# Two PSUM banks for the low-rank product, two copying engines, and gate and up in turns at the block heads

## The chip, the cores and the metric

The kernel runs on one NeuronCore of a Trainium2 chip. The metric is the device time of one execution in microseconds. Before the change it is 483.63 us (median of three runs, 483.47 to 484.6). The profile of one of these executions has a span of 481.9 us; times within the kernel count from the start of that span. The engines are TensorE (PE; its weight loads are PEld), VectorE (DVE), ScalarE (ACT), GpSimd (POOL) and SyncE (SP), which issues nearly all transfers.

## The reference

For each of 8 batches of 256 tokens of width 1024 there is an adapter, one of eight, picked by an index. It is a low-rank product: x times B (to 16 numbers per token), and that times A (back to 1024). Its result goes through a feed-forward part with fp8 rounding and comes back as an addition to x.

```python
Bx  = einsum('bni,bri->bnr', x, B[ids])        # 1024 -> 16
y   = einsum('bnr,bor->bno', Bx, A[ids])       # 16 -> 1024
q   = fp8(y / in_scale) * in_scale
hidden = silu(q @ gate.T * s_g) * (q @ up.T * s_u)    # 1024 -> 2752
return x + fp8(hidden / s_in) @ down.T * s_d           # 2752 -> 1024
```

All inputs are float32; the weights of gate, up and down already lie on the fp8 grid.

## The kernel before

The 2048 tokens are cut into four blocks `t` of 512 (two batches each), the 1024 inputs into eight slices `k` of 128, the 2752 hidden units into 22 chunks `c` of 128 (the last has 64). Everything lies transposed: features on partitions, tokens along the free axis. Products land in PSUM, of which a pool of eight banks (tag `ps`) hands out one at a time. Three stages follow each other.

**Low-rank product.** For blocks 0 and 1 `two_times_b` (line 445) forms B's product `bx` for a block: at each of the eight `k`, four matmuls of 128 tokens each go to the four groups of 32 rows of one bank; rows 0 to 63 hold one batch and rows 64 to 127 the other. Then `bx` is copied to SBUF as `bm`: one copy of all rows by DVE (line 454), and four copies of 16 rows, each into its neighbour's group of rows, two by DVE and two by ACT (line 459). `two_times_a` (line 470) multiplies by A in two parts. Each part fills four banks `c0` to `c3` with 16 matmuls (a float32 matmul leaves two records in the trace), the first eight with the plain copy and the others with the shifted ones. Each full bank is rounded to fp8 into `xg` by `round_to`: two banks by ACT (line 468) and two by DVE (line 466). A bank can be used again once it has been rounded. Blocks 2 and 3 share `four_times_b` and `four_times_a`, with 256 tokens a matmul.

**Gate and up.** `gate_up(c, t)` (line 519) runs eight matmuls of 512 tokens for gate and eight for up, each eight into a bank of its own (`y0`, `y1`), then ACT's SiLU on gate and DVE's multiplication with up (line 548), whose result is `hid`. For blocks 0 and 1 the slices `k` are taken in the order in which they are rounded:

```python
ORDER = [0, 1, 4, 5, 2, 3, 6, 7]
```

`between` is called after gate's matmuls and `halfway` after four of up's. Lines 571 to 593 use them to weave the low-rank product of the next block into gate and up of this one. `pass_time` runs matmuls on zeros so that TensorE doesn't stand still at the start.

**Down.** 22 chunks are summed into the output, x is added, and the block is written (lines 643 to 675).

**What sets the order.** Every engine works through its own queue in order. `multiply` and the copies are held in program order; the other instructions are placed by the tile layer, which also puts in the waits: a reader waits for the writer, a new user of a bank for its last reader, and an instruction of one engine for those of other engines on the same bank, reads included. SyncE issues the loads in the order of lines 343 to 369 and 598; the first chunk of `w_gu` is behind x of block 0, then come the other three of the first four chunks, block 1's adapters and x in two halves, and blocks 2 and 3.

Of the kernel before, what the change touches and what calls it, by code (L numbers as in the profile page):

```python
# [2 lines left out]

# [5 lines left out]
F32 = mybir.dt.float32  # L9
# [8 lines left out]
P = 128  # L18
T = 2048
SEQ = 256  # L20
# [3 lines left out]
R = 16  # L24
NH = H // P
NI = (I + P - 1) // P
TAIL = I - (NI - 1) * P
TB = 512
# [5 lines left out]
ORDER = [0, 1, 4, 5, 2, 3, 6, 7]  # L34
# [11 lines left out]
def high(ap):  # L46

    return ap.bitcast(BF16)[..., 1::2]
# [205 lines left out]
def adaln_ffn(  # L254
# [13 lines left out]
    nc = tc.nc  # L268
    const = ctx.enter_context(tc.tile_pool(name="const", bufs=1))
    psum = ctx.enter_context(  # L270
        tc.tile_pool(name="psum", bufs=8, space=bass.MemoryType.PSUM)
    )
# [16 lines left out]
    with ExitStack() as fast:  # L289
        acts = fast.enter_context(tc.tile_pool(name="acts", bufs=1))  # L290
        lora = fast.enter_context(tc.tile_pool(name="lora", bufs=1))
# [5 lines left out]
        xg = [acts.tile([P, NH, TB], FP8, name=f"xg{t}") for t in range(NTB)]  # L297
# [9 lines left out]
        b_two = [lora.tile([P, 2 * BROW + R], F32, name=f"b{t}") for t in range(2)]  # L307
        a_two = [lora.tile([P, H // 2], F32, name=f"a{t}") for t in range(2)]

        b_four = lora.tile([P, 4 * BROW + R], F32, name="b_four")  # L310
# [109 lines left out]
        def multiply(*args, **kwargs):  # L420
            tc.keep_in_program_order(nc.tensor.matmul(*args, **kwargs))  # L421
# [3 lines left out]
            for i in range(n):  # L425
                multiply(to[:, :P], lhsT=zeros, rhs=zeros, start=(i == 0), stop=(i == n - 1))

        def times_b(b, n, quads, between=None):

            bx = psum.tile([P, n], F32, tag="ps", name="bx")  # L430
            for k in range(NH):
                for q, (t, i, cols) in enumerate(quads):
                    at = i * BROW + k * R
                    multiply(
                        bx[32 * q : 32 * (q + 1)],
                        lhsT=b[:, at : at + 32],
                        rhs=xs[t][:, k, cols],
                        start=(k == 0),
                        stop=(k == NH - 1),
                    )  # L440
                if between:
                    between(k)
            return bx

        def two_times_b(t, between=None):


            n = SEQ // 2
            quads = [(t, q // 2, bass.ts(q, n)) for q in range(4)]
            bx = times_b(b_two[t], n, quads, between)  # L450
            bm = [
                lora.tile([P, n], F32, tag=f"bm{i}", name=f"bm{i}", bufs=2) for i in range(3)
            ]
            tc.keep_in_program_order(nc.vector.tensor_copy(bm[0], bx))
            for q in range(4):
                to = bm[1 + q // 2][32 * q : 32 * q + R]
                other = bx[32 * (q ^ 1) : 32 * (q ^ 1) + R]
                tc.keep_in_program_order(
                    nc.vector.tensor_copy(to, other) if q < 2 else nc.scalar.copy(to, other)  # L459
                )  # L460
            return bm

        def round_to(to, c, engine):
# [6 lines left out]
        def two_times_a(t, bm):  # L470

            n = SEQ // 2
            for part in range(2):
                cs = [psum.tile([P, 2, SEQ], F32, tag="ps", name=f"c{q}") for q in range(4)]
                for other in range(2):
                    for i in range(2):
                        for q in range(4):
                            rows = slice(32 * q, 32 * q + R)
                            multiply(
                                cs[q][:, i, bass.ts(q % 2 ^ other, n)],  # L480
                                lhsT=a_two[t][rows, bass.ts(2 * part + i, P)],
                                rhs=bm[other * (1 + q // 2)][rows],
                                start=True,
                                stop=True,
                            )
                for q in range(4):
                    k = 4 * (q % 2) + 2 * part
                    to = xg[t][:, k : k + 2, bass.ts(q // 2, SEQ)]
                    round_to(to, cs[q], nc.vector if q // 2 else nc.scalar)

        def four_times_b():
            quads = [(2 + q // 2, q, bass.ts(q % 2, SEQ)) for q in range(4)]
            bx = times_b(b_four, SEQ, quads)
            bm = lora.tile([P, SEQ], F32, tag="bm", name="bm", bufs=2)
            nc.vector.tensor_copy(bm, bx)
            return bm

        def four_times_a(bm, pairs):
            for i in pairs:
                cs = [psum.tile([P, 2, SEQ], F32, tag="ps", name=f"c{q}") for q in range(4)]  # L500
                for k in range(2):
                    for q in range(4):
                        rows = slice(32 * q, 32 * q + R)
                        multiply(
                            cs[q][:, k],
                            lhsT=a_four[rows, bass.ts(2 * i + k, P)],
                            rhs=bm[rows],
                            start=True,
                            stop=True,
                        )  # L510
                for q in range(4):
                    to = xg[2 + q // 2][:, 2 * i : 2 * i + 2, bass.ts(q % 2, SEQ)]
                    round_to(to, cs[q], nc.vector if q % 2 else nc.scalar)
# [2 lines left out]
            return slice(0, TAIL) if t % 2 else slice(TAIL, P)  # L516


        def gate_up(c, t, between=None, halfway=None):
            tail = c == NI - 1  # L520
            w = w_of[c]
            cols = bass.ts(t, TB)
            ys = []
            for j in range(1 if tail else 2):
                y = psum.tile([P, TB], F32, tag="ps", name=f"y{j}")
                order = ORDER if t < 2 else range(NH)
                for i, k in enumerate(order):
                    if halfway and j and i == NH // 2:
                        halfway()
                    multiply(  # L530
                        y,
                        lhsT=high(w[:, j * NH + k, :]),
                        rhs=xg[t][:, k, :],
                        start=(k == order[0]),
                        stop=(k == order[-1]),
                    )
                ys.append(y)
                if between and not j:
                    between()
            gates, ups = (ys[0], ys[-1]) if not tail else (ys[0][:TAIL], ys[0][TAIL:])  # L540
            rows = slice(TAIL, P) if tail else slice(0, P)
            if tail:
                to = lora.tile([P, 2 * TB], FP8, tag="bm", name="tail", bufs=2)[half_of(t), :TB]
            else:
                to = hid[c][:, cols]
            g = work.tile([P, TB], F32, tag="g", name="g")
            nc.scalar.activation(g[rows], gates, AF.Silu, scale=gate_s[: gates.shape[0]])  # L547
            nc.vector.scalar_tensor_tensor(  # L548
                to,
                in0=ups,  # L550
                scalar=up_by_down[rows],
                in1=g[rows],
                op0=ALU.mult,
                op1=ALU.mult,
                saturate=False,
            )
            if tail:
                nc.vector.tensor_copy(hid_tail[half_of(t), t // 2], to)
            if c > 1 and t == (NTB - 1 if c < 4 else 1):
                for done in {2: (0, 2), 3: (1, 3)}.get(c, (c,)):  # L560
                    note_low_bits(w_of[done], P, done)
                if c <= 1 + 2 * NTB:
                    i, half = divmod(c - 2, 2)
                    ks = slice(half * NH // 2, (half + 1) * NH // 2)
                    note_squares(xg[i][:, ks, :], P, c - 2)
                for done in (0, 1) if c == 2 else (c - 1,):
                    note_squares(hid[done], P, 2 * NTB + done)
# [5 lines left out]
        bm = two_times_b(0, lambda k: pass_time(warm, 6) if k in (3, 5) else None)  # L573
        pass_time(warm, 8)
        two_times_a(0, bm)
        for c in range(3):
            gate_up(c, 0)
        bms = []
        gate_up(
            3,  # L580
            0,
            between=lambda: bms.append(two_times_b(1)),
            halfway=lambda: two_times_a(1, bms[0]),
        )
        for c in range(2):
            gate_up(c, 1)
        gate_up(
            2,
            1,
            between=lambda: bms.append(four_times_b()),  # L590
            halfway=lambda: four_times_a(bms[1], (0, 1)),
        )
        gate_up(3, 1, between=lambda: four_times_a(bms[1], (2, 3)))
        for c in range(4):
            for t in (2, 3):
# [47 lines left out]
        for k in range(NH):  # L643
            ws = []
            for half in range(2):
                n = HALF - half
                w = wpool.tile([P, 2 * NH, P], F32, tag="w", name="w_d")[:, :n]
# [9 lines left out]
            for t in range(NTB):  # L657
                for c in range(NI - 1):
                    nc.tensor.matmul(  # L659
                        ys[t],  # L660
                        lhsT=high(ws[c]),
# [95 lines left out]
```

## Time and profile before

| | us |
|---|---|
| time, median of three | 483.63 |
| span of the profile | 481.9 |
| PE busy | 473.1 (98%) |
| ACT busy | 192.3 (40%) |
| DVE busy | 105.5 (22%) |
| one gate or up matmul, mean record | 0.379 |
| one rounding: ACT (line 468), DVE (line 466) | 0.686, 0.746 |
| copy of 16 rows: ACT, DVE (line 459) | 0.257, 0.281 |
| SiLU, multiplication into hid | 0.681, 0.751 |

A matmul's record of 379 ns is its latency. Matmuls overlap, so a row of them advances faster than that. Busy shares are means over the three stages; what an edit can do is read from the stretch where it works, here the first 56 us. The chain of waits goes back from the last instruction to what released each step, and shows which engine set the pace at each time.

### The profile page before, as it was taken

How to read it: one execution, taken by the hardware profiler on the slowest of the kernel's cores; microseconds unless marked ns; L12 is line 12 of the kernel's file. 1: busy time of each engine (PE TensorE's matmuls, PEld its weight loads, DVE VectorE, ACT ScalarE, POOL GpSimd, SP SyncE). 2: the span in 40 equal slices, each digit the busy share in tenths (PEclk: the TensorE clock that was granted, in tenths of full speed). 3: DMA queues.
4: the chain of work that ended last, by engine and by line, in shares of the span. 5: the costliest groups of instructions: out<-in, count | busy, mean ns of one | idle time of the engine just before them, and what ended most of it. 6: DMA issues, size and time to landing. Idle time of an engine off the chain costs nothing.

```text
span 481.9 us, 6062 instructions
## 1 busy us (share of the span) xinstructions
PE 473.1 (98%) x2550; PEld 221.3 (46%) x2550; DVE 105.5 (22%) x165; ACT 192.3 (40%) x247; POOL 0.2 (0%) x4
## 2 busy tenths in 40 slices
PE   8999999999999999999999999999999999999994
PEld 7554544444444444444444444444444444444442
DVE  1341521212121212121212121232120120111021
ACT  1331517995556654433454544359112112011000
POOL 0000000000000000000000000000000000000000
PEclk9999999999999999999999999999999999999999
DMA  8997004522221122222211111111434335242031
GB/s 287 418 345 243 1 0 148 194 97 88 87 88 48 46 82 89 87 87 88 87 37 52 45 60 55 61 54 62 151 116 137 115 131 158 76 170 99 0 133 50
DMA packets 13173, 52.67 MB, mean 109 GB/s; under 512 B 1554, under 2 KB 2578, under 8 KB 9554
## 3 DMA queue, kind: packets, MB, share of 16 engines
q1 hardware_dynamic: 12992, 52.14, 31.9%
q8 instruction: 22, 0.36, 0.3%
q14 instruction: 13, 0.11, 0.1%
q10 hardware_dynamic: 146, 0.07, 0.0%
HBM read 43.81 MB, written 8.39 MB: 108 GB/s over the span
## 4 chain that ended last, share of the span: by engine, by line
PE 95%; DVE 0%; ACT 0%; issue 0%
PE y L421 62%; PE yd L659 30%; PE c L421 1%; PE bx L421 1%; PE yd L627 1%; ACT xg L468 0%; DVE o L637 0%; DVE xg L466 0%; PE count L618 0%
## 5 line engine op out<-in xcount | busy, mean ns | idle before, releaser
L421 PE MATMUL y<-xg,w_gu 128*128 128x512 fp8e4 x1376 | 298.5, 379 | 0.1
L421 PEld LDWEIGHTS <-w_gu 128*128 128x128 bf16 x1376 | 133.9, 98 | 163.2 <-DVE xg L466 1.5
L659 PE MATMUL yd<-hid,w_d 128*128 128x512 fp8e4 x672 | 146.1, 379 | 0.0
L547 ACT ACTIVATE g<-y,gate_s 128x512 f32<-128x512 f32 (+1 forms) x88 | 59.8, 681 | 139.5 <-PE y L421 139.5
L548 DVE SCALAR_TENSOR_TENSOR hid<-y,up_by_down,g 128x512 fp8e4<-128x512 f32 x84 | 63.1, 751 | 218.5 <-PE y L421 153.5
L659 PEld LDWEIGHTS <-w_d 128*128 128x128 bf16 x672 | 65.3, 98 | 79.9 <-issue 1.7
L407 ACT ACTIVATE junk<-w_d 128x1408 bf16<-128x1408 uint16 (+1 forms) x16 | 21.2, 1324 | 88.5 <-DMA w_d<-w_d 88.4
L637 DVE SCALAR_TENSOR_TENSOR o<-yd,down_s,x 128x512 f32<-128x512 f32 x32 | 23.0, 748 | 118.1 <-PE yd L627 62.4
L407 ACT ACTIVATE junk<-w_gu 128x2048 bf16<-128x2048 uint16 (+1 forms) x22 | 41.0, 1864 | 0.1
L414 ACT ACTIVATE junk<-hid 128x2048 bf16<-128x2048 fp8e4 x21 | 40.0, 1905 | 0.4
L414 ACT ACTIVATE junk<-xg 128x2048 bf16<-128x2048 fp8e4 x8 | 15.2, 1905 | 0.2
L468 ACT ACTIVATE xg<-c,inv 128x512 fp8e4<-128x512 f32 x16 | 9.9, 686 | 7.2 <-PE c L421 7.2
L466 DVE TENSOR_SCALAR xg<-c,inv 128x512 fp8e4<-128x512 f32 x16 | 11.1, 746 | 6.6 <-PE c L421 6.5
L421 PE MATMUL warm<-zeros 128*128 128x128 bf16 x84 | 8.0, 278 | 1.0 <-DVE zeros L279 1.0
L421 PEld LDWEIGHTS <-zeros 128*128 128x128 bf16 x84 | 7.3, 131 | 1.6 <-DVE zeros L279 1.0
L421 PE MATMUL c<-bm,a 16*128 16x128 f32 x128 | 5.4, 287 | 0.6 <-ACT xg L468 0.6
L459 ACT COPY bm<-bx 16x128 f32<-16x128 f32 x4 | 1.0, 257 | 12.0 <-DMA w_gu<-w_gu 9.8
L421 PEld LDWEIGHTS c<-bm,a 16*128 16x128 f32 x128 | 4.8, 185 | 1.3 <-ACT xg L468 0.7
L421 PE MATMUL c<-bm,a_four 16*128 16x256 f32 x64 | 4.7, 394 | 0.3 <-ACT xg L468 0.3
L421 PE MATMUL bx<-x,b 128*32 128x128 f32 x128 | 4.3, 275 | 0.7 <-DMA x<-x 0.4
L407 ACT ACTIVATION_READ_ACCUMULATOR junk<-w_gu 128x1 f32 x22 | 4.2, 191 | 0.0
L627 PE MATMUL yd<-hid_tail,w_dt 64*128 64x512 bf16 x32 | 4.2, 379 | 0.0
(41 smaller groups left out, 35.5 us busy)
## 6 DMA issues: line engine op xcount, KB each, us to landing
w_gu<-w_gu SPq DMA_DIRECT2D x21, 1024.0 KB, 4.9
outT<-o SPq DMA_DIRECT2D x32, 256.0 KB, 2.3
x<-x SPq DMA_DIRECT2D x7, 1024.0 KB, 10.4
w_d<-w_d SPq DMA_DIRECT2D x8, 704.0 KB, 4.6
w_d<-w_d SPq DMA_DIRECT2D x8, 640.0 KB, 3.8
x<-x SPq DMA_DIRECT2D x2, 512.0 KB, 6.0
a<-a SPq DMA_DIRECT2D x4, 128.0 KB, 6.0
w_dt<-w_d_tail SPq DMA_DIRECT2D x2, 256.0 KB, 11.5
```

What stands on the lines that cost most here:

```text
L407: nc.scalar.activation(junk_like(w), low(w), AF.Copy, accum_out=lows[:rows, column : column + 1])
L414: nc.scalar.activation(junk_like(q), q, AF.Square, accum_out=squares[:rows, column : column + 1])
L421: tc.keep_in_program_order(nc.tensor.matmul(*args, **kwargs))
L459: nc.vector.tensor_copy(to, other) if q < 2 else nc.scalar.copy(to, other)
L466: nc.vector.tensor_scalar(to, c, scale, None, ALU.mult, saturate=False)
L468: nc.scalar.activation(to, c, AF.Copy, scale=scale, saturate=False)
L547: nc.scalar.activation(g[rows], gates, AF.Silu, scale=gate_s[: gates.shape[0]])
L548: nc.vector.scalar_tensor_tensor(to, in0=ups, scalar=up_by_down[rows], in1=g[rows], op0=ALU.mult, op1=ALU.mult, saturate=False,)
L627: nc.tensor.matmul(ys[t], lhsT=high(wt[half_of(t), k, :]), rhs=hid_tail[half_of(t), t // 2], start=start, stop=not start,)
L637: nc.vector.scalar_tensor_tensor(o, in0=y, scalar=down_s, in1=xs[t][:, k, :], op0=ALU.mult, op1=ALU.add)
L659: nc.tensor.matmul(ys[t], lhsT=high(ws[c]), rhs=hid[c][:, bass.ts(t, TB)], start=(first and c == 0), stop=(not first and c == NI - 2),)
```

## The change

It has three parts.

1. In `two_times_b` each batch's B product gets a bank of its own. DVE copies the one and ACT the other, plain and shifted copies alike: three copies on each engine, without a bank in common.
2. `gate_up` has a switch `paired`. With it, gate and up take turns at each `k`, so that both use a freshly rounded slice before the next is needed. It is on for the first chunk of blocks 0 and 1. The banks of gate and up are now both taken at the start.
3. `halfway` is gone: `two_times_a(1)` and the first half of `four_times_a` come after all of up's matmuls, not after the first four.

The low-rank product of blocks 2 and 3 keeps its single bank and single copy. The core of the diff:

```diff
-        def times_b(b, n, quads, between=None):
-
-            bx = psum.tile([P, n], F32, tag="ps", name="bx")
+        def times_b(bx, b, n, quads, between=None):
+
             for k in range(NH):
                 for q, (t, i, cols) in enumerate(quads):
                     at = i * BROW + k * R
                     multiply(
-                        bx[32 * q : 32 * (q + 1)],
+                        bx[q][32 * q : 32 * (q + 1)],
...
-            bx = times_b(b_two[t], n, quads, between)
+            bx = [psum.tile([P, n], F32, tag="ps", name=f"bx{j}") for j in range(2)]
+            times_b([bx[q // 2] for q in range(4)], b_two[t], n, quads, between)
             bm = [
-                lora.tile([P, n], F32, tag=f"bm{i}", name=f"bm{i}", bufs=2) for i in range(3)
+                lora.tile([P, 2, n], F32, tag=f"bm{j}", name=f"bm{j}", bufs=2) for j in range(2)
             ]
-            tc.keep_in_program_order(nc.vector.tensor_copy(bm[0], bx))
-            for q in range(4):
-                to = bm[1 + q // 2][32 * q : 32 * q + R]
-                other = bx[32 * (q ^ 1) : 32 * (q ^ 1) + R]
-                tc.keep_in_program_order(
-                    nc.vector.tensor_copy(to, other) if q < 2 else nc.scalar.copy(to, other)
-                )
+            for j, copy in enumerate((nc.vector.tensor_copy, nc.scalar.copy)):
+                rows = slice(64 * j, 64 * (j + 1))
+                tc.keep_in_program_order(copy(bm[j][rows, 0], bx[j][rows]))
+                for q in (2 * j, 2 * j + 1):
+                    other = 32 * (q ^ 1)
+                    tc.keep_in_program_order(
+                        copy(bm[j][32 * q : 32 * q + R, 1], bx[j][other : other + R])
+                    )
...
-                                rhs=bm[other * (1 + q // 2)][rows],
+                                rhs=bm[q // 2][rows, other],
...
-        def gate_up(c, t, between=None, halfway=None):
+        def gate_up(c, t, between=None, paired=False):
+
...
-            ys = []
-            for j in range(1 if tail else 2):
-                y = psum.tile([P, TB], F32, tag="ps", name=f"y{j}")
-                order = ORDER if t < 2 else range(NH)
-                for i, k in enumerate(order):
-                    if halfway and j and i == NH // 2:
-                        halfway()
...
+            js = range(1 if tail else 2)
+            ys = [psum.tile([P, TB], F32, tag="ps", name=f"y{j}") for j in js]
+            order = ORDER if t < 2 else list(range(NH))
+            for j, k in [(j, k) for k in order for j in js] if paired else product(js, order):
+                multiply(
+                    ys[j],
...
         for c in range(3):
-            gate_up(c, 0)
+            gate_up(c, 0, paired=(c == 0))
         bms = []
-        gate_up(
-            3,
-            0,
-            between=lambda: bms.append(two_times_b(1)),
-            halfway=lambda: two_times_a(1, bms[0]),
-        )
+        gate_up(3, 0, between=lambda: bms.append(two_times_b(1)))
+        two_times_a(1, bms[0])
         for c in range(2):
-            gate_up(c, 1)
-        gate_up(
-            2,
-            1,
-            between=lambda: bms.append(four_times_b()),
-            halfway=lambda: four_times_a(bms[1], (0, 1)),
-        )
+            gate_up(c, 1, paired=(c == 0))
+        gate_up(2, 1, between=lambda: bms.append(four_times_b()))
+        four_times_a(bms[1], (0, 1))
         gate_up(3, 1, between=lambda: four_times_a(bms[1], (2, 3)))
```

More of the change, by code (lines that the diff above doesn't have):

```diff
@@ L1 @@
 from contextlib import ExitStack
+from itertools import product
 from math import prod
@@ L442, in times_b @@
                     between(k)
-            return bx
         def two_times_b(t, between=None):
@@ L492, in four_times_b @@
             quads = [(2 + q // 2, q, bass.ts(q % 2, SEQ)) for q in range(4)]
-            bx = times_b(b_four, SEQ, quads)
+            bx = psum.tile([P, SEQ], F32, tag="ps", name="bx")
+            times_b([bx] * 4, b_four, SEQ, quads)
             bm = lora.tile([P, SEQ], F32, tag="bm", name="bm", bufs=2)
@@ L522, in gate_up @@
             cols = bass.ts(t, TB)
-            ys = []
-            for j in range(1 if tail else 2):
-                y = psum.tile([P, TB], F32, tag="ps", name=f"y{j}")
-                order = ORDER if t < 2 else range(NH)
-                for i, k in enumerate(order):
-                    if halfway and j and i == NH // 2:
-                        halfway()
[L530 to L535, printed above, removed]
-                    )
-                ys.append(y)
-                if between and not j:
+            js = range(1 if tail else 2)
[4 more added lines that the diff above has]
+                    ys[j],
+                    lhsT=high(w[:, j * NH + k, :]),
+                    rhs=xg[t][:, k, :],
+                    start=(k == order[0]),
+                    stop=(k == order[-1]),
+                )
+                if between and (j, k) == (0, order[-1]):
                     between()
@@ L576, in adaln_ffn @@
         for c in range(3):
-            gate_up(c, 0)
+            gate_up(c, 0, paired=(c == 0))
         bms = []
-        gate_up(
-            3,
-            0,
-            between=lambda: bms.append(two_times_b(1)),
-            halfway=lambda: two_times_a(1, bms[0]),
-        )
-        for c in range(2):
-            gate_up(c, 1)
-        gate_up(
-            2,
-            1,
-            between=lambda: bms.append(four_times_b()),
-            halfway=lambda: four_times_a(bms[1], (0, 1)),
-        )
+        gate_up(3, 0, between=lambda: bms.append(two_times_b(1)))
+        two_times_a(1, bms[0])
+        for c in range(2):
+            gate_up(c, 1, paired=(c == 0))
+        gate_up(2, 1, between=lambda: bms.append(four_times_b()))
+        four_times_a(bms[1], (0, 1))
         gate_up(3, 1, between=lambda: four_times_a(bms[1], (2, 3)))
```

## The prediction

> **What bounds the kernel now.** I read the page first, then the chain of waits from 7 to 56 us, then the order in time inside the few microseconds where that chain leaves TensorE, then the landing of the loads.
>
> ```profile
> PE 473.1 (98%) x2550; PEld 221.3 (46%) x2550; DVE 105.5 (22%) x165; ACT 192.3 (40%) x247; POOL 0.2 (0%) x4
> PEclk9999999999999999999999999999999999999999
> DMA  8997004522221122222211111111434335242031
> ```
>
> TensorE is busy for 98% of the span at full clock, so little can be won anywhere, and only where TensorE stands still. In this row of 40 slices of 12 us DMA is nearly full in the first four and idle in the next two. All code that the diff touches runs before 56 us.
>
> ```profile
> 15.64 0.67 DVE xg L466
> 16.31 0.05 issue
> 16.36 10.97 PE y L421 x50
> 27.32 1.88 PE bx L421 x64
> 29.21 0.97 PE y L421 x4
> 30.18 1.25 PE c L421 x30
> 31.43 0.68 ACT xg L468
> 32.10 0.04 issue
> 32.15 1.15 PE c L421 x26
> 33.30 9.60 PE y L421 x44
> 42.90 3.59 PE bx L421 x64
> 46.49 0.97 PE y L421 x4
> 47.46 1.11 PE c L421 x16
> 48.58 0.68 ACT xg L468
> ```
>
> Columns are start, length, work. The chain leaves TensorE at three junctions, where B's product, A's product and the rounding to fp8 (lines 466 and 468) meet gate and up. At 16.3 us TensorE waits for roundings; at 31.4 and 48.6 us the A product of the second half waits for a PSUM bank that a rounding has to empty first. From 50 us on the chain is TensorE alone (415.00 us busy in the stretch 55 to 470).
>
> ```profile
> 11.35 0.29 DVE L454 COPY bm<-bx 128x128 f32<-128x128 f32 x1 [3.22 <-PE bx L421]
> 11.67 0.59 DVE L459 COPY bm<-bx 16x128 f32<-16x128 f32 x2
> 12.36 0.54 ACT L459 COPY bm<-bx 16x128 f32<-16x128 f32 x2 [9.75 <-DMA w_gu<-w_gu]
> 13.57 2.73 DVE L466 TENSOR_SCALAR xg<-c,inv 128x512 fp8e4<-128x512 f32 x4 [1.31 <-PE c L421]
> ```
>
> ACT's two copies start 0.1 us after DVE's last one ends (11.67 + 0.59 = 12.26), though B's product has been there since 11.35: five copies run one after the other, to 12.90. The bracket blames an older DMA; the summed waits put 2.2 us of the other instance on DVE's copy of line 459.
>
> [...] ACT's copies queue behind DVE's of line 459 too, which read other quadrants. [...] here the roundings run side by side, four in 2.42 us on ACT and four in 2.73 on DVE. [...] the trace has 10.97 us for 50, 219 ns, and 216 between weight loads.
>
> **The change part by part.** Junction by junction; each inherits the lead of the one before.
>
> *First junction (c = 0, block 0).* The product goes to two banks; DVE copies one (a 64-row copy and two of 16 rows), ACT the other. DVE still ends at 12.26 (the 128-row copy took 291 ns, a 16-row one 281, so fewer rows save nothing). ACT's three start near 11.40 and take 257 ns at a pitch of 0.28: end 12.22. The unknown is ACT's 64-row copy; no row shows it. By the 16-row row it costs 0.26, and 128x512 took 0.69, so at most 0.4 more than I take; I take 0.26. The last copy comes 12.90 - 12.26 = 0.64 sooner, the A products and roundings about 0.61 sooner. Gate would start at 14.48 - 0.61 = 13.87; its weights landed at 13.76, so they just do not hold it.
> Before, gate's pairs of k started at 14.48, 15.03, 15.69 and 16.35, each held by a DVE rounding (2.73 us for four), and up followed: 16.45 + 10 x 0.216 = 18.6 at the end of c = 0. Gate and up in turns have four matmuls per pair, 0.86 us, more than a rounding's 0.67, so no later pair waits. One new wait: up's first matmul, now second in the queue, takes the bank of the second ACT rounding (end 14.75 - 0.61 = 14.14), so it goes at about 14.34 with the handover, with everything behind it. End: 14.34 + 15 x 0.216 = 17.6. Gain 1.0 us.
>
> *But block 1's x.* B's product for block 1 would start at 27.25 - 1.0 = 26.2 and want the second half of x1 four k later, at 27.1. It was issued at 11.52 and its landing is the longest here:
>
> ```profile
> L330 SPq DMA_DIRECT2D x<-x x2: 339/366/392, 11.1 to 11.5; - x2
> DMA to landing us min/median/max: 13.2/14.6/16.1
> ```
>
> 11.52 + 16.1 = 27.62. Nothing that the diff touches moves this: the queue's instructions keep their order and TensorE gates none of those loads. Before, it was wanted at 28.04. So all but about 0.4 us of the first gain is given back here. I carry 0.4.
>
> *Second junction (gate_up(3, 0), the A product of block 1, gate_up(0, 1)).* The halfway insertion goes: up's eight matmuls run at once and then the 64 A records without a break. Before: from up's first weight load at 29.14 to the end of gate_up(0, 1), 33.33 + 20 x 0.216 = 37.65: 8.51 us. After: eight up matmuls to the last load 1.31, the switch to A as before 0.52, 16 groups of four records at 0.11 = 1.65 (the copies are done at 29.5, over a microsecond before), the switch back 0.31, 0.1, and 16 matmuls 3.46: 7.35, plus 0.1 for up's first matmul behind the second ACT rounding. Gain 8.51 - 7.45 = 1.06. It consists of 0.34 us in which A waited for the ACT copies and 0.82 for the bank.
> What is added: hid's multiplication (line 548, 0.75 us) for up of c = 3 now stands on DVE ahead of the four roundings, and the fourth A tile of the second half takes up's bank and waits for it. It starts some 0.05 us before the A product does and is over in 0.8; the first DVE rounding can't start before 1.05 us after A's start, and that tile's first matmul is due at 0.9. Both are hidden, just.
>
> *Third junction (gate_up(2, 1), gate_up(3, 1)).* The same with 256 columns. Before, from 46.42 to up's load at 54.99 8.57 us, with 32 A records from 47.39 to 49.84, 2.44 us; the second lot of 32 took 1.42 (53.05 to 54.47), having no such wait. After, both take 1.42: gain 1.0. Gate of (3, 1) waits for the first ACT rounding, done 1.85 us after A's start, when 1.94 are due. Second-half x3 landed at 42.18 and is wanted at 44.37 - 1.5 = 42.9: no stall.
>
> *Costed at nothing*: the four extra copies in two_times_b (within the parallel ones), the early allocation of up's tile (eight banks are enough, and after 56 us the order on every engine is the same), the B product spread over two banks (A's products already rotate over four at a group of 0.11 us).
>
> *Sum*: 0.4 + 1.06 + 1.0 = 2.5 us. TensorE is the chain for all of the rest, and the next load after 39 us is issued at 78.5, on the release of a buffer, so the lead is kept to the end: 483.63 - 2.5 = 481.1.
>
> **Rivals.**
> (a) *x1 doesn't hold.* Its landing is made by DMA that is full until 46 us; if it comes 0.6 us sooner, the first gain counts in full: 483.63 - 3.1 = 480.5. Against: 27.62 is what this trace has.
> (b) *A new wait eats one junction.* The margins on DVE and on the banks are 0.1 us. If one of them fails, hid's 0.75 us goes in front of the roundings and one junction is nearly lost, and up's first matmul waits longer too: about 1.3 left, 482.3.
> (c) *Nothing gained.* The loads decide all junctions, x3 too, or the roundings without gate matmuls to cover them are exposed for 0.7 to 0.8 us at each: 483.6. Against: x3 had 0.7 us to spare even with the lead.
> (d) *Slower.* If a matmul that alternates between two accumulating banks can't hide its weight load, 32 x 98 ns = 3.1 us; with hid exposed twice (1.5) the change costs 4.6 and gains 2.5: 485.7. For it: no row shows 512-column matmuls in turns on two banks. Against: the weights alternate in every pair already, and A's products rotate banks at full rate.
>
> **How the numbers follow.** Forecast 0.64, (a) 0.10, (b) 0.14, (c) 0.08, (d) 0.04. The range takes in (a) at 480.4 and reaches just over (b), to 482.4; (c) and (d) stay out. Faster by over 0.3% means below 482.2: forecast, (a) and a little of (b), 0.76; within, the rest of (b) and (c), 0.19; slower 0.05.
>
> **What will show it.** Right: ACT and DVE copies start within 0.1 us of each other at 11.4; c = 0 ends near 17.6 instead of 18.6; a wait on x in the middle of block 1's B product, which ends only 0.4 us sooner; both "ACT xg" pieces of the chain at 31.4 and 48.6 gone; everything after 56 us 2.5 us sooner with equal lengths. Wrong: a landing of x1 far from 27.6, hid's multiplication ending after the first A rounding could start, a y matmul at more than 220 ns where gate and up alternate, or a stall on a bank in the second half of A.

## The result, and the profile after

The changed kernel takes 481.72 us (median of six runs, 481.44 to 483.57), the kernel before 484.16 beside it (six runs): a ratio of 0.9957, 95% interval 0.9937 to 0.9977. The forecast was 481.1, range 480.4 to 482.4; it counted from the 483.63 of the three earlier runs. The profiled execution has a span of 479.6 us instead of 481.9.

The chain of waits of the changed kernel, from 11 to 53 us (start, length, work):

```profile
11.17 16.47 DMA x<-x
...
27.68 1.08 PE bx L422 x32
28.76 1.83 PE y L422 x8
30.60 2.07 PE c L422 x64
32.66 0.34 PE y L422
33.00 0.03 issue
33.03 8.58 PE y L422 x39
41.61 3.59 PE bx L422 x64
45.20 1.83 PE y L422 x8
47.03 2.04 PE c L422 x32
49.07 1.83 PE y L422 x8
50.91 1.94 PE c L422 x32
```

Both pieces "ACT xg" are gone, and so is DVE's rounding at 16 us. In their place stands one transfer: x of block 1, issued at 11.17, on which TensorE waits in the middle of block 1's B product. The 64 records of A's product (line 422 of the changed kernel) take 2.07 us in one piece.

In order of time (start, length, engine, work, idle before and what ended it):

```profile
10.77 0.28 DVE L456 COPY bm<-bx 64x128 f32<-64x128 f32 x1 [3.16 <-PE bx L422]
10.82 0.26 ACT L456 COPY bm<-bx 64x128 f32<-64x128 f32 x1 [8.22 <-PE bx L422]
...
14.01 0.82 PE L422 MATMUL y<-xg,w_gu 128*128 128x512 fp8e4 x3 [0.67 <-DMA w_gu<-w_gu]
...
27.68 0.81 PEld L422 LDWEIGHTS bx<-x,b 128*32 128x32 f32 x32 [0.67 <-DMA x<-x]
...
30.70 0.75 DVE L547 SCALAR_TENSOR_TENSOR hid<-y,up_by_down,g 128x512 fp8e4<-128x512 f32 x1 [1.00 <-PE y L422]
```

The copies start 0.05 us apart, and ACT's 64-row copy costs 0.26. Gate waits 0.67 us for its weights at 14.01. The second half of block 1's x holds TensorE for 0.67 more; up's matmuls stand behind it in the queue and, though they read nothing of it, start only at 28.69. The multiplication into hid runs from 30.70 to 31.45, beside A's product.

For comparing kernels I use four marks, all starts of weight loads: m1 of block 1's B product, m2 of the first up matmul behind it, m3 of the B product of blocks 2 and 3, m4 of the first up matmul behind the last A product. x1 is the second transfer of x of block 1. From m4 to the first down matmul every trace of this study has 270.89 us, and 149.36 from there to the last matmul: nothing after m4 changes. Executions differ in when the loads land (x1 from 27.60 to 28.20 in the table), so m3 - m2 and m4 - m3 compare better than times do. In the table, parts 1, 2 and 3 are those of the section on the change; all numbers are us.

| | m1 | m2 | m3 - m2 | m4 - m3 | m4 | x1 landed |
|---|---|---|---|---|---|---|
| before | 27.25 | 29.14 | 13.70 | 12.16 | 54.99 | 27.62 |
| the change | 26.20 | 28.69 | 12.85 | 11.24 | 52.77 | 27.64 |
| part 1 alone | 26.33 | 28.85 | 15.28 | 12.16 | 56.28 | 27.80 |
| part 2 alone | 26.57 | 29.25 | 13.70 | 12.16 | 55.11 | 28.20 |
| part 3 alone | 27.09 | 29.06 | 13.34 | 11.64 | 54.04 | 28.01 |
| without part 1 | 26.18 | 29.20 | 12.85 | 11.24 | 53.29 | 28.14 |
| without part 2 | 26.16 | 28.65 | 13.34 | 11.24 | 53.23 | 27.60 |
| without part 3 | 26.38 | 29.05 | 15.27 | 12.16 | 56.48 | 27.99 |

The change's lead at m4 is 0.45 + 0.85 + 0.92 = 2.2 us.

The ratios below are to the kernel before, run beside each on the same chip. Medians of different chips are not compared: the kernel before alone has 485.03, 484.91 and 483.99 on the three that were used.

### The profile page after: what moved, and what is told of

Read it like the earlier page. It is cut to its first block, busy times and chain, and to the rows that moved or that the text cites. A ratio compares the mean times of both kernels' runs of the same rounds, so it can differ in the third digit from the quotient of the medians.

```text
span 479.6 us, 6067 instructions
## 1 busy us (share of the span) xinstructions
PE 470.7 (98%) x2550; PEld 219.9 (46%) x2550; DVE 105.4 (22%) x165; ACT 192.6 (40%) x249; POOL 0.2 (0%) x4
## 4 chain that ended last, share of the span: by engine, by line
PE 93%; DMA 4%; SPq 2%; issue 0%; DVE 0%
PE y L422 60%; PE yd L650 30%; DMA x<-x 3%; PE c L422 1%; PE bx L422 1%; PE yd L618 1%; SPq L317 0%; SPq L339 0%; SPq L331 0%; SPq L320 0%; SPq L325 0%; DMA ids_i<-ids 0%; DVE o L628 0%; PE count L609 0%
## 5 line engine op out<-in xcount | busy, mean ns | idle before, releaser
L422 PEld LDWEIGHTS bx<-x,b 128*32 128x32 f32 x128 | 3.2, 109 | 2.3 <-DMA x<-x 1.2
L422 PE MATMUL c<-bm,a 16*128 16x128 f32 x128 | 4.3, 278 | 0.0
```

## Experiments: one part alone

**Part 1 alone** (two banks, copies on both engines; the rest as before).

```diff
+            bx = [psum.tile([P, n], F32, tag="ps", name=f"bx{j}") for j in range(2)]
...
+            for j, copy in enumerate((nc.vector.tensor_copy, nc.scalar.copy)):
```

> Part 1 alone (two banks, DVE and ACT copy at once). Marks: m1 the first load of block 1's B product (before 27.25, after the change 26.20), m2 the first up load behind it (29.14; 28.69), m3 the first load of the B product of blocks 2 and 3 (42.83; 41.54), m4 the first up load behind the last A product (54.99; 52.78). Theory (x1's landing caps the first junction, the copies count at the second only because up's four matmuls don't cover them, the bank wait stays): m1 0.5 to 0.6 us sooner, m2 only 0.4 sooner, m3 - m2 shorter by 0.34, m4 - m3 as before; 0.7 us in all, 483.4. Rival (the copies are the gain, 0.64 at each of two junctions): 1.2 us, 482.9.

Measured: 484.02 us, ratio 0.9989 (0.9976 to 1.0003), which is not to be told from no change. m1 is 0.92 sooner, but m2 only 0.29: x1 landed at 27.80 here. m3 - m2 came out longer, for a reason that is not part 1's alone: 7 of its 20 executions, and 12 of 49 of the kernel before beside it, have a mean granted clock of 0.994 or less. TensorE's granted clock in three stretches of this trace (length, busy and instructions, clock, DMA share, GB/s):

```profile
29.70:33.10 3.40, 2.86 (x67) 1.00 1.06 287
33.10:36.60 3.50, 3.50 (x10) 0.51 1.04 400
36.60:40.00 3.40, 3.40 (x17) 1.00 1.00 300
```

For 3.41 us the clock is halved (0.51 is the mean of the middle row), which costs 1.7: the 44 matmuls of gate and up behind A's product take 11.29 us here and 9.60 in the kernel before. Without it m3 - m2 is 13.57: 0.13 shorter, not 0.34. Ahead of the halved stretch the trace shows the same: from m2 to the first gate load behind A's product it is 3.99 us instead of 4.09. The trace of the kernel before tells why it isn't 0.34. There, apart from the wait for the bank, the groups of four loads in A's product of block 1 follow each other every 0.11 us, and one of them, waiting for ACT's copies, after 0.22; so that wait cost 0.1. The rival is refuted: 0.64 is kept at neither junction.

**Part 2 alone** (turns; `halfway` kept).

```diff
-            gate_up(c, 0)
+            gate_up(c, 0, paired=(c == 0))
...
-            gate_up(c, 1)
+            gate_up(c, 1, paired=(c == 0))
```

> Part 2 alone (gate and up in turns for the first chunk of blocks 0 and 1; halfway kept). Theory: m1 0.45 us sooner, all of it kept at m2 but no more since x1 then just holds (0.4), m3 - m2 and m4 - m3 as before, since with halfway kept the four up matmuls already cover the roundings of block 1: 0.4 us in all, 483.7. Rival (turns hide roundings at both heads, 0.5 to 0.6 each): 1.1 us, 483.0.

Measured: 484.35 us, ratio 0.9992 (0.9976 to 1.0008), again not to be told from no change. m1 is 0.68 sooner, and x, landing at 28.20, took all of it: m2 is 0.1 later than before. m3 - m2 is 13.70 as before: with halfway kept, turns bring nothing at block 1.

**Part 3 alone** (A's product unbroken, no turns, one bank).

```diff
-            halfway=lambda: two_times_a(1, bms[0]),
...
+        two_times_a(1, bms[0])
...
-            halfway=lambda: four_times_a(bms[1], (0, 1)),
...
+        four_times_a(bms[1], (0, 1))
```

> Part 3 alone (up's eight matmuls at once, then A's product without a break). Theory: m1 and m2 as before; m3 - m2 shorter by 0.45 only, because without turns gate of (0, 1) waits for each of block 1's roundings; m4 - m3 shorter by 0.92, as with the whole change: 1.4 us in all, 482.8. Rival (the breaks were only idle time that moves elsewhere): m4 at 54.9, no change.

Measured: 482.71 us, ratio 0.996 (0.9938 to 0.9983). m3 - m2 shrinks by 0.36; the chain shows what is left over:

```profile
30.97 1.23 PE c L421 x32
32.19 2.72 DVE xg L466 x4
34.96 7.51 PE y L421 x34
42.47 3.99 PE bx L421 x64
```

Four DVE roundings, 2.72 us, now set the pace. m4 - m3 misses 0.4 of the 0.92: the B product took 3.99 instead of 3.59, since the last x landed at 44.50 in this execution (42.58 with the whole change). So m4 is 0.95 sooner and not 1.4, and x of block 3 can hold too. Without that wait this part alone would bring 0.36 + 0.92 of the 0.85 + 0.92 us that the whole change gains at the second and third junctions.

## Experiments: one part left out

**Without part 1** (one bank, five copies one after the other).

> The whole change without part 1 (one bank, copies one after the other). Theory: m1 0.5 us sooner than before instead of 1.05, m2 still 0.4 sooner, since x1's landing decides; m3 and m4 as with the whole change, since eight up matmuls (1.7 us) cover the five copies (1.6 us). So the change's first part brings nothing here: 2.2 us sooner than before at m4, 481.8. Rival (the copies are needed at both junctions): m4 1.0 to 1.2 us later than with the whole change, 482.9.

Measured: 481.93 us, ratio 0.9945 (0.9924 to 0.9967). m3 - m2 and m4 - m3 are those of the whole change to 0.01 us, though the copies run one after the other again. m1 is 26.18, as with the whole change and not 0.5 later. The first gate load is at 13.90 here, right behind A's product, and at 14.00 with the whole change, whose early copies gate could not use because its weights landed at 13.96. m2 follows from x (28.14), so m4 is 1.7 sooner than before and not 2.2. In the whole change with x as four and four slices, part 1 brings nothing that these runs show; with six and two, where the weights came sooner (below), leaving it out was not run.

**Without part 2.**

```diff
-            gate_up(c, 1, paired=(c == 0))
+            gate_up(c, 1)
```

(and the same at block 0)

> The whole change without part 2 (gate first, then up, everywhere). Theory: m1 0.5 to 0.9 us sooner than before, m2 0.4 sooner; m3 - m2 0.5 longer than with the whole change, since gate of (0, 1) now waits for each rounding on DVE; m4 - m3 equal: m4 1.7 us sooner than before, 482.3. Rival (turns are idle decoration once the copies are early): as the whole change, 481.7.

Measured: 482.4 us, ratio 0.9955 (0.994 to 0.997). m2 28.65, m3 - m2 13.34, 0.49 longer than with the whole change, m4 - m3 equal: as the theory said, with m4 1.76 sooner than before for 1.7. Turns are worth 0.5 us at the second junction, and only behind an unbroken A product.

**Without part 3** (A's product again after four of up's matmuls).

> The whole change without part 3 (A's product again after four of up's matmuls). Theory: m2 0.4 us sooner than before; the bank wait of 0.82 us is back at the second junction and 0.9 at the third, so m3 - m2 is shorter by 0.3 alone and m4 - m3 as before: m4 0.75 us sooner than before, 483.4. Rival (the parts are about equal): m4 1.5 us sooner, 482.6.

Measured: 483.67 us, ratio 0.9975 (0.9964 to 0.9986). m3 - m2 is 15.27 with 3.41 us at half clock from 33.43 on (the 44 matmuls take 11.29 us again); without its 1.7 us it is 13.57, 0.13 shorter than before, as with part 1 alone. m4 - m3 is 12.16, as before. Less the 1.7 us, m4 is 0.2 sooner than before; 0.75 was expected, but x1 landed at 27.99 and left 0.1 of the lead at m2, and the copies brought 0.13 for 0.3. Both bank waits are back, so the third part is what removes them.

## Experiments: the transfer that now holds

**x of block 1 as six and two slices**, in the changed kernel and in the kernel before.

```diff
-        load_x(1, 0, 4)
-        load_x(1, 4, 4)
+        load_x(1, 0, 6)
+        load_x(1, 6, 2)
```

> The whole change, with x of block 1 loaded as six and two slices instead of four and four: the same bytes in the same place of the queue, but slices 4 and 5 land before the B product wants them. Theory (x1's landing takes 0.6 us of the first junction's 1.05): block 1's B product starts as with the change (26.2), waits for slice 6 for 0.2 us or less, m2 at 28.3 instead of 28.69, m4 and the end 0.4 us sooner than with the whole change: 481.3. Rival (the wait is paid back later anyway, or slice 0 now comes too late): m4 as with the whole change or later, 481.7.

Measured: 481.76 us, ratio 0.9947 (0.9927 to 0.9967). The chain of this trace has the B product in one piece, with no transfer in it:

```profile
26.13 1.95 PE bx L422 x64
28.08 1.83 PE y L422 x8
```

m2 is 28.01, 0.68 sooner than with four and four; m3 - m2 and m4 - m3 are unchanged, and m4 is 52.10. Of the 0.68, 0.14 comes from an earlier m1 (26.06) and 0.54 from the wait that is gone. The median of six doesn't show it: the interval of this ratio overlaps that of the change (0.9937 to 0.9977).

> The kernel before, with x of block 1 loaded as six and two slices. Theory: without the change the B product of block 1 never waited for x, so nothing moves at any mark: 484.1. Rival (the split itself is better or worse for the queue): 0.3 us or more either way.

Measured: 483.76 us, ratio 0.9984 (0.997 to 0.9998): 0.8 us sooner where nothing was expected. The trace can't say why, as it has 6.83 us at half clock from 12.85 on (a mean of 0.51 from 12.80 to 19.70), which puts m1 at 29.75, after every load. The kernel before wanted the second half at 28.04, and it landed between 27.60 and 28.20 in the traces of four and four so far. That it can hold there too, the trace of part 3 alone shows, whose code up to this product is that of the kernel before:

```profile
28.05 0.81 PEld L421 LDWEIGHTS bx<-x,b 128*32 128x32 f32 x32 [0.15 <-DMA x<-x]
```

These 0.15 us are less than 0.8; where the rest comes from stays open.

**The change again, and two steps further.** First the changed kernel, beside the other two on one chip.

> The changed kernel itself, beside the next three and a kernel before of the same chip. Two of the traces so far have a window of 3.41 us at half clock at 33 us (the change's first part alone, and the whole change without its third); both keep the break in A's product. If the break makes such windows, this kernel has none after 20 us and its executions lie close together (within 1.5 us), while those of the kernel before spread over 3 us or more; if the windows come by chance, it spreads like the kernel before. Marks otherwise: m2 28.7, m3 - m2 12.85, m4 - m3 11.24; 481.7.

Measured: 482.5 us over 22 runs (481.59 to 485.05), ratio 0.9969 (0.9956 to 0.9982). There is no stretch at half clock after 20 us in this trace, but the executions spread over 3.5 us, like those of the kernel before (482.97 to 486.31). The expectation of a narrow spread failed. x1 landed at 28.27, m2 was 29.33, and TensorE waited 1.1 us for it; so it came later than the 29.14 of the kernel before. m3 - m2 and m4 - m3 are 12.85 and 11.24 again.

Then the turns two slices at a time, on six and two:

```diff
+            pairs = [order[i : i + 2] for i in range(0, NH, 2)]
+            turns = [(j, k) for ks in pairs for j in js for k in ks]
-            for j, k in [(j, k) for k in order for j in js] if paired else product(js, order):
+            for j, k in turns if paired else product(js, order):
```

> The whole change with x of block 1 as six and two slices, and the turns taken two slices at a time (gate, gate, up, up), so that up's first matmul comes third and not second. Theory (up's first matmul waits 0.2 us for the bank of the second ACT rounding at the second junction): m2 at 28.0 to 28.3 as with six and two alone, m3 - m2 12.65 instead of 12.85, m4 - m3 11.24: 0.6 to 0.9 us sooner than the whole change, 481.0. Rival (the wait only moves to another slice): m3 - m2 12.85, 481.2.

Measured: 480.95 us (six runs, 480.56 to 482.34), ratio 0.9929 (0.9905 to 0.9952), the lowest median of all, against 482.5 for the change on this chip. m3 - m2 is 12.66: up's first matmul, now third, waits no longer, and the piece of 0.34 us is gone from the chain:

```profile
30.24 2.07 PE c L422 x64
32.30 8.76 PE y L422 x40
41.06 3.88 PE bx L422 x64
```

m2 is 28.33 and m4 52.52. The second transfer of x of block 1, now two slices, landed at 27.72 and held the product again:

```profile
27.76 0.38 PEld L422 LDWEIGHTS bx<-x,b 128*32 128x32 f32 x16 [0.49 <-DMA x<-x]
```

So six and two slices do not take this wait away in every execution. The 3.88 has 0.3 us of waiting for the last x in it: the next load in line.

Last, on top of that, the first chunk's weights in two transfers, slices 0 and 1 first:

```diff
-        load_gate_up(0)
...
+        for ks in (slice(0, 2), slice(2, NH)):
+            nc.sync.dma_start(
+                out=w.rearrange("p (j k) n -> p j k n", j=2)[:, :, ks],
...
```

> As the one before, and the weights of the first chunk come in two transfers, slices 0 and 1 of gate and up first. Theory (in the changed kernel the first gate matmul at 14.00 waits for these weights, which landed at 13.96, and not for the rounding, done at 13.27): first gate matmul at 13.4, 0.4 to 0.6 sooner; then x of block 1 holds again, because block 1's B product asks at 25.5 for slices that land near 26, so at m2 only 0 to 0.3 us of it is left: 480.8. Rival (kilobyte pieces slow the queue): first gate matmul not sooner, m2 later than 28.3, 481.5.

Measured: 482.28 us, ratio 0.9956 (0.9937 to 0.9975). The first gate matmul starts at 13.27, 0.7 us sooner than in the changed kernel and 0.4 sooner than without the split, so its weights did hold it there. But nothing of it arrives:

```profile
11.50 14.94 DMA x<-x
...
26.58 2.15 PE bx L428 x63
```

The B product now waits for its first slices until 26.44, and m2 is 28.66. Without the split they landed at 25.77. The extra transfer stands ahead of them in the queue: x of block 1 was issued at 11.50 instead of 10.77, and landed as much later. From issue to landing it took 14.94 us for 15.00, so the slow queue of the rival is not seen. Its m2 later than 28.3 came, although gate did start sooner, and the median is above the 480.95 without the split.

## Why the prediction was right

*Direction and sum.* 2.5 us were forecast; m4 shows 2.2, the first pair of medians 2.4, the second pair 1.5. The steps, one by one:

*First junction: the size came out by the cap, and in part by luck.* 0.4 us was carried and 0.45 measured at m2. The copies end 0.65 us sooner relative to the product, as worked out (0.90 us after it for 1.55). The step "its weights landed at 13.76, so they just do not hold it" failed: they landed at 13.96, the first slices were rounded by 13.27, and gate waited 0.67. m1 is 1.05 sooner all the same, but half of that is this execution's, in which the last x of block 0 landed at 10.04 instead of 10.59. Counted from the first load of block 0's A product, m1 comes after 14.98 us instead of 15.49. With six and two slices, where gate's weights landed at 13.58, it comes after 14.47: there the 1.0 us that was worked out is seen. It changed nothing at m2, because x1 took the lead anyway: 27.64 for the 27.62 worked out. That these two agree so closely is luck, as x1 landed up to 0.65 later in other traces, and with 28.27 m2 was 0.2 later than in the trace before. Likewise the wait of up's first matmul did not show at this junction; the weights covered it.

*Second junction: mechanism right, 1.06 forecast, 0.85 measured.* Two terms were small by about 0.1 each. Up's first matmul waits 0.2 behind the second ACT rounding, not 0.1; taking that wait away gave 0.19. And A's product took 0.1 longer than its 1.65. That figure is fifteen steps of 0.11 and not the sixteen groups it names, and the fourth tile's first load came 0.08 late, behind hid's multiplication. This began 0.18 after the product and not 0.05 before it, and ended at 31.45; "both are hidden, just" was not quite so. The split into 0.34 for copies and 0.82 for the bank was wrong: the copies alone gave 0.13. The rest came from the unbroken product, as the kernel without part 3 shows.

*Third junction: 1.0 forecast, 0.92 measured.* A's first lot took 1.52 for the 1.42: the fourth tile waits for hid's multiplication, which ends at 47.89.

*Kept to the end.* Right: 270.89 and 149.36 us in all traces.

*Rivals.* (a) was wrong for the change, but the trace of six and two slices shows what it described, with m4 2.9 us sooner than before. (b), (c) and (d) did not come, though one margin that (b) named was overrun by the 0.08 us above. Against (d): the 39 matmuls from 33.03 on, the first 15 of them in turns on two banks, take 8.58 us, 220 ns each.

*Left open.* The executions of one kernel spread over up to 4.5 us. Two causes are seen in traces: landings (x1 from 27.60 to 28.27, the last x from 42.18 to 44.50) and stretches at half clock. Whether the change makes such stretches rarer is not settled. The mean granted clock of each execution bears on it: traces without such a stretch have 0.996 or more, those with one 0.993, the one with twice that length 0.988. On the chip of the second pair 3 of 22 executions of the changed kernel and 5 of 31 of the kernel before are at 0.994 or less, so such stretches probably come with an unbroken product too. They do not make the gain, though: among the executions at 0.996 or more the medians are 482.28 and 483.67, and 1.4 of the 1.5 us remain.

## What to carry to other kernels

Where the busiest engine pauses for a buffer, look first at what broke its work into pieces: here an uninterrupted product removed both bank waits, because other work before it gave the copies their time and work after it, in turns, gave the roundings theirs. Parallel copies brought nothing in the whole change with four and four slices, where another wait ended later. And before a lead is counted, compare it with the landing of the next load in the queue, in more than one execution: a lead beyond that landing is waited away. Cutting that load differently took 0.54 us of waiting away in one trace and left 0.49 in the next, and starting gate 0.7 us sooner brought nothing.

## What was not expected of the hardware

In three traces TensorE's clock was granted at half, for 3.41 us (part 1 alone from 33.15, without part 3 from 33.43) or for 6.83 us (the kernel before with six and two, from 12.85), in the middle of a kernel whose TensorE is 98% busy. The stretches of 3.41 us begin 0.3 and 0.4 us after the first gate load behind the broken A product of block 1 (32.84 and 33.03), the one of 6.83 within block 0's product. Block 1's broken product is followed by full clock in the three other traces that have it: before, part 2 alone, and before with six and two (9.60 us for the 44 matmuls in each).

Why one execution has such a stretch and the next has not, no run here shows. The idle time does not tell these two apart: TensorE was busy 2.86 of the 3.40 us ahead of the halved stretch in part 1 alone (29.70 to 33.10), and 2.85 of 3.40 in the kernel before (29.80 to 33.20), where the clock stayed full. One stretch of 3.41 us costs 1.7 us, nearly as much as the 2.2 us that the whole change gains, and a comparison of two single executions can be decided by it.
